# Second attention: PSUM banks dealt out anew, one for the projections and two for the maxima's scores

## The chip, the cores and the metric

The kernel runs on one core of one Trainium2 chip. A core has five engines that work side by side, each with its own queue that it takes in order: TensorE (PE in the profile; its weight loads are shown apart as PEld), VectorE (DVE), ScalarE (ACT), GpSimd (POOL), and SyncE (SP), which issues the DMAs here. Matmuls write to PSUM, which this program divides into eight banks of 128 partitions by 512 float32 values. A tile in a bank can be given to a new matmul when every instruction that reads the old tile is done.

The metric is the device time of the program in microseconds (us). Three runs of the kernel before took 915.53, 917.35 and 935.15 us; the median is 917.35.

## The reference

The program computes two transformer layers on x of 2 x 1024 x 128 in float32. Every sub-layer reads a layer norm of x, and its result is added to x:

```
x = x + attention0(ln(x))    # 16 heads of 8, softmax over 1024 keys
x = x + moe0(ln(x))          # 8 experts of 64, the best 2, and a shared expert
x = x + attention1(ln(x))    # 8 query heads, 4 key heads of 128, rotary, causal
x = x + moe1(ln(x))          # 16 experts of 128, the best 4
```

The change lies in attention1. Cut to what matters:

```
q = hidden @ Wq ; k = hidden @ Wk ; v = hidden @ Wv    # 8, 4 and 4 heads of 128
q = q * cos + rotate_half(q) * sin                     # k likewise
attn = softmax(causal(q @ k.T / sqrt(128)))            # two query heads share a key head
out  = (attn @ v) reshaped to (b, t, 1024) @ Wo
```

## The kernel before

**Stages.** The first attention takes the span up to some 370 us, the first feed-forward up to some 440, the second attention (`attn1`) up to some 805, and the second feed-forward the rest. They overlap at their ends: the scheduler moves independent work across.

**Units of the second attention.** For each batch b (2) and key head kv (4) there are four query chunks qc of 256 queries: 32 units, numbered 16 b + 4 kv + qc. Each unit serves the two query heads of its key head.

- *Projections* (`attn1_proj`, ten per key head): for each half i of the sequence one K (`kp`), two Q (`qp`), and two V (`vp`). `mm3` makes each float32 product out of three matmuls of high and low parts (its matmuls all have line 166). `vp` has six matmuls of 256 columns, since Wo has been multiplied into V's weights. K and Q go through `rope`: three VectorE operations read the projection's bank (lines 856 to 858), then GpSimd adds (859), ScalarE takes the high part (860), and GpSimd the low part (861). `vp` is copied to V by ScalarE (891).
- *Maxima* (`attn1_s`): for each of a unit's four pairs of query tile and head, one matmul per 512 keys writes scores to a tile `s` (915); VectorE reduces it to the row's maximum (920 for a part that isn't the last, 924 for the last with the causal mask). When the unit's four columns of m stand, `mt` turns them on TensorE (928). They reach the scores in one of two ways. In most units VectorE spreads them over rows (940), and a fourth matmul adds them to the scores (961). In the ten units of `APART` (3, 7, 14, 15, 22, 23, 26, 27, 30, 31) ScalarE copies them (931), one DMA stores them to memory (933), a second spreads them over all partitions (934), into `mb`, and VectorE subtracts `mb` from the scores (964).
- *Scores again, transposed* (`attn1_st`): for each key tile kt three matmuls to a tile `st` (954), the maxima as above, the exponential on ScalarE (966) into `pt`; on the diagonal GpSimd clears what is masked (970).
- *Products* (`attn1_av`): `pt` times V, with a column of ones that gives the sums, adds up in the tiles `o` (987), one for each query tile. At a tile's end come a reciprocal (994), ScalarE's scaling (998) and GpSimd's addition to x (1000).

**Order.** The loop in `attn1` emits this stepwise: one `st` step, then as many steps of the maxima's stream as keep it a fixed lead ahead (`lead < 13 + step*28//20`), then projections of the next key head by a rate, then one step of side work (weights and front ends of the second feed-forward), and the products one step late. From what is emitted, a scheduler makes each engine's own order, by its estimate of when operands and banks come free; only the first attention's TensorE order is fixed by hand (`manual_schedule`).

**PSUM banks in the second attention.** Eight banks are held by pools: `pst` has three, used by `pt(...)` for projections, `st`, `mt` and transposes in turn; `psy` has one (an `o` tile, later the feed-forward's sum); `a1s` has three for the maxima's scores; `a1o` has one for the other `o`. During the first feed-forward the four banks of `a1s` and `a1o` belong to its pool `f0u`.

The first five projections of the first key head are issued during the first feed-forward (`islice(g, 5)`).

Of the kernel before, what the change touches and what calls it, by code (L numbers as in the profile page):

```python
# [10 lines left out]
F32 = mybir.dt.float32  # L11
# [6 lines left out]
PSUM = bass.MemoryType.PSUM  # L18
# [6 lines left out]
CH = 512  # L25
# [13 lines left out]
def cols(t, w=128):  # L39
    return slice(t * w, (t + 1) * w)  # L40


def run(*gens):
    for g in gens:
        for _ in g:
            pass
# [26 lines left out]
class Net:  # L73
# [13 lines left out]
    def setup(self, ctx):  # L87
        nc = self.nc
        self.marks = {}
        self.fronts = set()  # L90
        self.nx = Counter()
        self.psu = None
        self.early = True
        self.const = self.pool(ctx, "const")
        self.small = self.pool(ctx, "small", 4)
        self.tok = self.pool(ctx, "tok", 2)
        self.hl = self.pool(ctx, "hl", 1)
        self.dram = self.pool(ctx, "dram", 2, DRAM)
        self.pst = self.pool(ctx, "pst", 3, PSUM)
        self.psy = self.pool(ctx, "psy", 1, PSUM)  # L100
        self.x = [self.const.tile([128, TPC, D], F32, name=f"x_{c}") for c in range(NCHUNK)]
        xin = self.a["x"].rearrange("(c t p) d -> c p t d", p=128, t=TPC)
        self.load_x = lambda c: nc.sync.dma_start(out=self.x[c], in_=xin[c])
        self.load_x(0)
        self.load_x(1)
        self.ident = self.const.tile([128, 128], F32, name="ident")
        make_identity(nc, self.ident)
        ones = self.tok.tile([128, CH], F32, tag="xT", name="ones")
        nc.vector.memset(ones, 1.0)
        self.zero = self.const.tile([128, 1], F32, name="zero")  # L110
        nc.vector.memset(self.zero, 0.0)
        self.ones_r = self.const.tile([128, 128], F32R, name="ones_r")
        nc.vector.tensor_copy(self.ones_r, ones[:, 0:128])
        self.ones = ones

    def pt(self, shape, name):
        return self.pst.tile(shape, F32, tag="t", name=name)
# [745 lines left out]
    def attn1_proj(self, b, kv, xh):  # L863
        nc, pp = self.nc, self.a1p
        K = [pp.tile([128, T], F32R, tag=f"K{k}", name=f"K{k}_{b}_{kv}") for k in range(2)]
        Q = [pp.tile([128, 2, T], F32R, tag=f"Q{k}", name=f"Q{k}_{b}_{kv}") for k in range(2)]
        V = pp.tile([128, 8, 2, 129], F32, tag="V", name=f"V_{b}_{kv}")

        def gen():
            nc.gpsimd.memset(V[:, :, :, 128:129], 1.0)  # L870
            for i in range(2):
                assert (b, i) in self.fronts
                xi = [w[:, i, :] for w in xh]
                p = self.pt([128, CH], f"kp_{b}_{kv}_{i}")
                self.mm3(p, [w[:, cols(kv)] for w in self.a1wk], xi)
                self.rope([w[:, cols(i, CH)] for w in K], p, i, f"k_{b}_{kv}_{i}")
                yield
                for h in range(2):
                    hh = 2 * kv + h
                    p = self.pt([128, CH], f"qp_{b}_{hh}_{i}")  # L880
                    self.mm3(p, [w[:, cols(hh)] for w in self.a1wq], xi)
                    self.rope([w[:, h, cols(i, CH)] for w in Q], p, i, f"q_{b}_{hh}_{i}")
                    yield
                for j in range(2):
                    p = self.pt([128, 2, 256], f"vp_{b}_{kv}_{i}_{j}")
                    for u in range(2):
                        self.mm3(
                            p[:, u, :], [w[:, i, cols(2 * j + u)] for w in xh], [w[:, kv, :] for w in self.a1wvo]
                        )
                    k0 = 4 * i + 2 * j  # L890
                    nc.scalar.copy(V[:, k0 : k0 + 2, :, 0:128], p.rearrange("p u (h d) -> p u h d", h=2))
                    yield

        return (K, Q, V), gen()

    def rows_apart(self, b, kv, qc):
# [311 lines left out]
def interleave(main, *sides, ratio=1):  # L1208
    s = Side()
    for g in sides:  # L1210
        s.add(g)
    for _ in main:
        s.step(ratio)
    s.drain()


def held(net, gen):
    while True:
        with ExitStack() as ctx:
            for ins in net.marks.values():  # L1220
                ctx.enter_context(net.tc.issue_after(ins.ins))
            if next(gen, gen) is gen:
                return
        yield


def later(gen, n):
    for _ in range(n):
        yield
    yield from gen  # L1230


def build(tc, aps, upto=4):
    n = Net(tc, aps)
    out = aps["out"].rearrange("(c t p) d -> c p t d", p=128, t=TPC)

    def dump():
        for c in range(NCHUNK):
            tc.nc.sync.dma_start(out=out[c], in_=n.x[c])

    with ExitStack() as ctx:
        n.setup(ctx)
        c1 = ctx.enter_context(ExitStack())
        cr = ctx.enter_context(ExitStack())
        n.f0wp = n.pool(cr, "f0w")
        w1 = n.attn1_weights(c1)
        with ExitStack() as c0:
            cb = c0.enter_context(ExitStack())
            n.attn0(
                c0, cb,  # L1250
                {266: lambda: w1, 456: lambda: n.ffn0_front(0, 1), 458: lambda: n.ffn0_front(2)}
                if upto > 1 else {},
            )
        if upto == 1:
            return dump()
        n.attn1_pools(c1)
        xh = [n.attn1_x(0), None]
        first, g = n.attn1_proj(0, 0, xh[0])
        n.f0k = n.pool(cr, "f0k", 1)
        gens = {"proj": islice(g, 5)}  # L1260
        for c in range(NCHUNK):
            gens[f"up{c}"] = n.ffn0_up(c)
            gens[f"down{c}"] = n.ffn0_down(c)
        gens["front3"] = n.ffn0_front(3)
        for i in range(2):
            gens[f"a1{i}"] = n.attn1_front(0, xh[0], i)
        with ExitStack() as c0:
            n.psu = n.pool(c0, "f0u", 4, PSUM)
            for word in ORDER.split():
                count, k = word.split("*")  # L1270
                for _ in range(int(count)):
                    next(gens[k], None)
            for k in gens:
                run(gens[k])
            n.psu = None
            n.early = False
        with ExitStack() as c2:
            with ExitStack() as c3:
                n.a1s = n.pool(c3, "a1s", 3, PSUM)
                n.a1o = n.pool(c3, "a1o", 1, PSUM)  # L1280

                def front1():
                    xh[1] = n.attn1_x(1)
                    yield from n.attn1_front(1, xh[1], 0)
                    yield from n.attn1_front(1, xh[1], 1)

                def weights1():
                    cr.close()
                    n.f1wp = n.pool(c2, "f1w")
                    yield from n.ffn1_weights()  # L1290

                plan = {10: [lambda: held(n, front1())]}
                if upto > 3:
                    plan[9] = [lambda: held(n, weights1())]
                    plan[18] = [lambda: n.ffn1_front(0)]
                    plan[21] = [lambda: n.ffn1_front(1)]
                    plan[30] = [lambda: later(n.ffn1_front(2), 3)]
                n.attn1(first, g, xh, plan)
            c1.close()
            if upto == 3:  # L1300
                return dump()
            wk1 = n.pool(c2, "f1k", 2)
            pu = n.pool(c2, "f1u", 4, PSUM)
            interleave(n.ffn1_back(0, wk1, pu, out), n.ffn1_front(3), ratio=1)
            run(n.ffn1_back(1, wk1, pu, out))
            run(n.ffn1_back(2, wk1, pu, out), n.ffn1_back(3, wk1, pu, out))
# [67 lines left out]
```

## Time and profile before

| | |
|---|---|
| median of three runs | 917.35 us (915.53 to 935.15) |
| profiled execution | 920.4 us, its span 918.7 us |
| TensorE busy | 882.5 us (96%) |
| VectorE busy | 795.8 us (87%) |
| ScalarE busy | 603.1 us (66%) |
| GpSimd busy | 307.7 us (33%) |
| mean granted clock of TensorE | 0.973 |
| DMA | 49.11 MB, mean 53 GB/s |

The profile is of one execution. A line such as `L964 DVE TENSOR_TENSOR pt<-st,mb` names the source line, the engine, the operation, and what it writes and reads. `A <- B: 3.0, 4, 2.2` in a list of waits says that A stood idle until B was done: 3.0 us in total, in 4 places, 2.2 us the longest. A matmul's busy time includes the filling of the array, so that matmuls which follow each other overlap in the records; the chain of waits shows them without that overlap. A float32 product `o` stands as two records, a product of high and low parts as one.

### The profile page before, as it was taken

To read this page: it belongs to the slowest core of one execution; us is meant where nothing else is said; L and a number is where in the kernel's file an instruction comes from. 1 tells how busy PE (TensorE), PEld (TensorE's weight loads), DVE (VectorE), ACT (ScalarE), POOL (GpSimd) and SP (SyncE) were. 2 spreads that over 40 slices of the span, in tenths; PEclk is the share of its full clock that TensorE was granted. 3 is DMA by queue.
4 is the path that set the end of the run, shared out by engine and by line. 5 is a ranking of instruction groups with operands and counts; after the bars stand their busy time and mean duration, and the time that the engine had idled before them with its cause. 6 is when DMAs were issued, how large, how long until landed. Compare 5 with 4: busy or idle time off the path is not lost.

```text
span 918.7 us, 17141 instructions
## 1 busy us (share of the span) xinstructions
PE 882.5 (96%) x6449; PEld 596.5 (65%) x6449; DVE 795.8 (87%) x1636; ACT 603.1 (66%) x1159; POOL 307.7 (33%) x392
## 2 busy tenths in 40 slices
PE   7999999999999999998899998999999989999997
PEld 5544444444443443467789897988888979866775
DVE  7899999999997998568787788899979996799987
ACT  5578998988986897864445545444445444578775
POOL 2620000000100000034664657375737463245331
PEclk9999999999997997899999999999999999999999
DMA  5890100011000000032000001000000000055462
GB/s 159 244 317 5 45 3 2 1 47 59 22 27 1 1 1 1 3 127 83 1 13 1 13 26 44 1 25 1 2 1 26 12 15 13 24 196 161 140 200 74
DMA packets 32043, 49.11 MB, mean 53 GB/s; under 512 B 4544, under 2 KB 10488, under 8 KB 31960
## 3 DMA queue, kind: packets, MB, share of 16 engines
q1 hardware_dynamic: 31960, 48.03, 16.2%
q8 instruction: 50, 0.82, 0.4%
q14 instruction: 33, 0.27, 0.1%
HBM read 38.36 MB, written 9.65 MB: 52 GB/s over the span
## 4 chain that ended last, share of the span: by engine, by line
PE 69%; DVE 15%; ACT 6%; issue 4%; POOL 2%; DMA 2%; SPq 0%; DVEq 0%; POOLq 0%; ACTq 0%
PE av L463 15%; PE st L443 13%; PE o L987 10%; PE st L954 8%; ACT pt L449 3%; PE s L915 3%; PE f1y L166 3%; PE f1p L166 2%; PE f0y L777 2%; PE st L961 2%; PE vp L166 1%; PE qp L166 1%; DVE s L924 1%; PE hot L410 1%; PE avt L484 1%
## 5 line engine op out<-in xcount | busy, mean ns | idle before, releaser
L404 DVE TENSOR_REDUCE mx<-s 128x2 f32<-128x1024 f32 x256 | 299.5, 1220 | 18.8 <-PE s L398 15.5
L449 ACT ACTIVATE pt<-st 128x512 f32<-128x512 f32 x476 | 252.5, 602 | 39.4 <-PE s L398 28.0
L463 PE MATMUL av<-pt,V 128*32 128x256 f32 x2048 | 169.3, 410 | 0.0
L987 PE MATMUL o<-V,pt 128*128 128x129 f32 x1152 | 156.3, 275 | 2.9 <-ACT pt L966 1.8
L398 PE MATMUL s<-KS,QM 24*128 24x512 f32 x512 | 156.0, 512 | 0.9 <-DVE KS L330 0.7
L987 PEld LDWEIGHTS o<-V,pt 128*128 128x128 f32 x1152 | 148.8, 191 | 11.6 <-ACT pt L966 2.3
L443 PE MATMUL st<-QX,KS 25*128 25x512 f32 x476 | 147.1, 513 | 1.6 <-DVE a1wvo L161 0.6
L954 PE MATMUL st<-Q,K 128*128 128x512 f32 (+1 forms) x480 | 136.1, 391 | 6.0 <-DVE rB_q L858 3.0
L443 PEld LDWEIGHTS st<-QX,KS 25*128 25x128 f32 x476 | 63.4, 188 | 101.8 <-ACT pt L449 50.4
L492 POOL TENSOR_TENSOR x<-x,ov 128x128 f32<-128x128 f32 x16 | 7.3, 455 | 284.4 <-DVE ov L489 284.4
L954 PEld LDWEIGHTS st<-Q,K 128*128 128x128 f32 x480 | 79.4, 189 | 17.9 <-DVE rB_q L858 4.8
L966 ACT ACTIVATE pt<-st 128x512 f32<-128x512 f32 x88 | 47.8, 545 | 59.5 <-PE st L961 50.2
L463 PEld LDWEIGHTS av<-pt,V 128*32 128x32 f32 x2048 | 43.2, 111 | 65.6 <-issue 62.4
L966 ACT ACTIVATE pt<-pt 128x512 f32<-128x512 f32 x72 | 43.3, 603 | 53.1 <-DVE pt L964 52.6
L398 PEld LDWEIGHTS s<-KS,QM 24*128 24x128 f32 x512 | 66.4, 187 | 10.8 <-DVE mx L404 5.4
L1000 POOL TENSOR_TENSOR x<-x,w 128x128 f32<-128x128 f32 x128 | 59.4, 464 | 27.6 <-ACT w L998 23.5
L915 PE MATMUL s<-K,Q 128*128 128x512 f32 (+2 forms) x192 | 63.2, 356 | 0.8 <-DVE m L924 0.7
L998 ACT ACTIVATE w<-o,rz 128x128 f32<-128x128 f32 x128 | 40.0, 365 | 34.2 <-DVE rz L994 31.1
L166 PE MATMUL f1y<-f1s,f1w 128*128 128x512 f32 x192 | 55.8, 412 | 3.9 <-POOL f1s L161 2.4
L964 DVE TENSOR_TENSOR pt<-st,mb 128x512 f32<-128x512 f32 x72 | 46.3, 646 | 9.9 <-PE st L954 6.0
L1177 DVE SCALAR_TENSOR_TENSOR f1f<-f1f,f1gb 128x512 f32<-128x512 f32 x64 | 48.4, 773 | 6.3 <-ACT f1f L1176 5.6
L970 POOL TENSOR_SCALAR_AFFINE_SELECT pt<-pt 128x256 f32<-128x256 f32 x64 | 26.5, 417 | 80.2 <-ACT pt L966 80.1
(238 smaller groups left out, 1554.0 us busy)
## 6 DMA issues: line engine op xcount, KB each, us to landing
f1gb<-f1gd SPq DMA_DIRECT2D x64, 256.0 KB
f0gb<-f0gd SPq DMA_DIRECT2D x32, 128.0 KB
kd<-k SPq DMA_DIRECT2D x12, 256.0 KB
qd<-q SPq DMA_DIRECT2D x12, 256.0 KB
QM<-qd SPq DMA_DIRECT2D x3, 1024.0 KB
mb<-md SPq DMA_DIRECT2D x10, 256.0 KB
KS<-kd SPq DMA_DIRECT2D x2, 1024.0 KB
KS<-kd SPq DMA_DIRECT2D x2, 768.0 KB
```

What stands on the lines that cost most here:

```text
L166: self.nc.tensor.matmul(out, lhsT=lhs[l], rhs=rhs[r], start=start and i == 0, stop=stop and i == 2)
L398: self.last_s = nc.tensor.matmul(ps[:, k, :], lhsT=QM[c][r, g, cols(t)], rhs=KS[c // 2][r, g, cols(h, CH)], start=True, stop=True)
L404: self.marks["V"] = nc.vector.tensor_reduce(mxs[n][:, h, 2 * pr : 2 * pr + 2, t : t + 1], ps, AX.X, ALU.max, negate=True)
L443: nc.tensor.matmul(ps, lhsT=KS[c // 2][32 * j : 32 * j + 25, g, cols(kt)], rhs=QX[n][32 * j : 32 * j + 25, :], start=True, stop=True,)
L449: self.marks["A"] = nc.scalar.activation(e, ps, AF.Exp, scale=INV_SQRT_D)
L463: return nc.tensor.matmul(avs[n][cols(j, 32), q], lhsT=V[c // 2][kt // 4][:, kt % 4, 4 * g + j, :], rhs=es[j][:, q], start=kt == 0 and i = ...
L915: nc.tensor.matmul(s[:, 0 : k1 - k0], lhsT=Q[0][:, h, cols(qt)], rhs=K[0][:, k0:k1], start=True, stop=True)
L954: k = nc.tensor.matmul(o, lhsT=K[l][:, cols(kt)], rhs=Q[r][:, :, q0 : q0 + w], start=i == 0, stop=apart and i == 2)
L966: k = nc.scalar.activation(e[:, :, 256 - w :], o, AF.Exp, scale=INV_SQRT_D)
L987: nc.tensor.matmul(acc[t][:, h, :], lhsT=e[:, h, cols(t)], rhs=V[:, kt, h, :], start=(kt == 0 and h == 0), stop=(kt == qt and h == 1),)
L1000: nc.gpsimd.tensor_add(xt, xt, w[:, h, :])
L1177: nc.vector.scalar_tensor_tensor(f, f, F7, gbs[e], ALU.min, ALU.mult)
```

## The change

Projections of the second attention that are emitted after the first feed-forward take their PSUM tiles from a new pool `a1q` with one bank. The pool `a1s` of the maxima's scores has two banks instead of three. The sum stays at eight. `st`, `mt` and the transposes stay in `pst` with its three banks, which no later projection shares. The first five projections are emitted before `a1q` exists and still use `pst`.

```diff
@@ setup
         self.psu = None
         self.early = True
+        self.a1q = None
@@ attn1_proj
+        def pt(shape, name):
+            return self.pt(shape, name) if self.a1q is None else self.a1q.tile(shape, F32, tag="p", name=name)
+
         def gen():
...
-                p = self.pt([128, CH], f"kp_{b}_{kv}_{i}")
+                p = pt([128, CH], f"kp_{b}_{kv}_{i}")
...
-                    p = self.pt([128, CH], f"qp_{b}_{hh}_{i}")
+                    p = pt([128, CH], f"qp_{b}_{hh}_{i}")
...
-                    p = self.pt([128, 2, 256], f"vp_{b}_{kv}_{i}_{j}")
+                    p = pt([128, 2, 256], f"vp_{b}_{kv}_{i}_{j}")
@@ build
-                n.a1s = n.pool(c3, "a1s", 3, PSUM)
+                n.a1s = n.pool(c3, "a1s", 2, PSUM)
+                n.a1q = n.pool(c3, "a1q", 1, PSUM)
                 n.a1o = n.pool(c3, "a1o", 1, PSUM)
```

Nothing else is edited. Every engine executes the same instructions as before; the scheduler, which knows the pools, sets them in another order from the end of the first feed-forward on.

## The prediction

> **What bounds the kernel now.** I read the page first, then busy time by stage, then who waited for whom inside the second attention, then the chain of waits.
>
> ```profile
> span 918.7 us, 17141 instructions
> ...
> PE 882.5 (96%) x6449; PEld 596.5 (65%) x6449; DVE 795.8 (87%) x1636; ACT 603.1 (66%) x1159; POOL 307.7 (33%) x392
> ```
>
> TensorE is the busiest engine, with VectorE behind it. Shares over a whole span mix stages, so the second attention is cut out (columns: stretch, length, busy us of PE, PEld, DVE, ACT, POOL, clock, DMA):
>
> ```profile
> 450.00:480.00 30.00, 29.43 (x185) 25.70 (x183) 24.54 (x59) 14.08 (x32) 21.42 (x27) 1.00 0.03 10
> 480.00:800.00 320.00, 310.09 (x2046) 278.12 (x2046) 273.55 (x740) 158.76 (x352) 178.69 (x260) 0.99 0.05 15
> ```
>
> PE is idle for 9.9 of 320 us: little is left to win here, while DVE, at 85%, has little room to be late. What PE waited for between 450 and 800 us (total, times, longest):
>
> ```profile
> PE st L954 <- DVE rB_q L858: 3.0, 4, 2.2
> PE st L954 <- ACT V L891: 1.7, 3, 0.9
> PE f1tp L170 <- DVE pt L964: 1.4, 1, 1.4
> PE o L987 <- ACT pt L966: 1.1, 1, 1.1
> PE st L954 <- DVE pt L964: 0.9, 1, 0.9
> ...
> PE qp L166 <- DVE rB_k L858: 0.6, 1, 0.6
> ```
>
> Rows one, two and the last are the shared `pst` banks: a tile waits until a projection's reader (VectorE's rope, ScalarE's copy into V) has left its bank. They come to 3.0 + 1.7 + 0.6 = 5.3 us. No row names a wait of PE for the maxima's scores.
>
> **How I count.** The change adds and removes no instruction; it changes which bank a tile gets, and so the order in which the scheduler puts the work. The changed program's order can be read. I lay PE's instructions out in that order and count the PE work between two tiles with these pieces of the chain (start, us, what):
>
> ```profile
> 525.51 0.71 PE vp L166 x6
> 526.22 0.70 PE st L954 x3
> ...
> 530.10 0.89 PE o L987 x8
> ```
>
> A 512-column matmul is thus 0.233 us, six of V 0.71, four whole products of `o` (two records each) 0.89. Where the work between two tiles of one bank is shorter than its reader needs, PE waits for the difference. The same count on the order of before shows how far to trust it.
>
> **Part 1, projections leave `pst`: minus 5.3 us.** `st` tiles and transposes now have all three banks. The 5.3 us above go. Next late on those tiles is the exponential, whose read (L966, mean 545 ns) the new order leaves ample work for, except in part 4.
>
> **Part 2, projections alone in one bank: plus 6.8 us.** Each projection waits until the one before it has been read. K's and Q's are read by three VectorE operations:
>
> ```profile
> L857 DVE TENSOR_TENSOR rB_q<-qp,sin x29: 692/692/695, 449.9 to 754.0; 64x512 f32<-64x512 f32 x29
> L858 DVE TENSOR_TENSOR rB_q<-qp,sin x29: 683/683/684, 450.6 to 754.7; 64x512 f32<-64x512 f32 x29
> L856 DVE TENSOR_TENSOR rA_q<-qp,cos x28: 661/680/693, 461.8 to 753.3; 128x512 f32<-128x512 f32 x28
> ```
>
> That is 0.68 + 0.69 + 0.68 = 2.06 us, 2.09 with the gaps between them. By the timeline the first began a median 0.55 us after the projection's last matmul (least 0.04, mean 0.95), so the bank is held 2.64 us (2.13 to 3.05) beyond it. In the new order the PE work between neighbouring projections falls short of 2.64 in 13 of 45 cases, by 10.3 us together (5.2 at 2.13, 16.9 at 3.05). The same count for before, with three shared banks, gives 5.0 us against 3.6 recorded (3.0 + 0.6). Two of them, 2.35 and 1.16, lie in the ramp before 450 us, where PE already sits out gaps of 0.4 to 1.3 us behind the first feed-forward; I take those as covered: 10.3 - 3.5 = 6.8. Without that cover it is 10.3. Behind a waiting projection in PE's queue stand `st` and `o`, so the wait stops everything. V's copies (0.59 us) are short once or twice: 0.3 us.
>
> **Part 3, maxima's scores in two banks: plus 1.0 us.** A score tile's bank is free when VectorE has reduced it, 0.28 to 0.76 us by width, once it comes to it. PE work between tile n and n+2 in the new order is short by 0.4 us in all if VectorE comes within 0.15 us, 2.2 within 0.5, 7.5 within 0.9 (the median delay of before, 0.86). For n and n+3 in the old order these counts are 0.6, 1.3 and 2.9, and the waits of PE show none; the weight loads (PEld) show 0.3. So VectorE is on time where it matters, and I take 1.0 net, between 0 and 7.
>
> **Part 4, the maxima come later: plus 5.7 us.** With two banks the scheduler sets each unit's scores later, and the transpose `mt` of its maxima closer to their use. For the ten units in `APART` the maxima go through memory before VectorE can subtract them. The last of these in before:
>
> ```profile
> 785.47 0.11 PE mt L928
> ...
> 787.12 3.61 DMA mb<-md
> ...
> 790.86 0.69 DVE pt L964
> ```
>
> From `mt` to this issue is 1.8 us; over the ten units 1.76 to 2.82, mean 2.25. With 3.61 for the landing the maxima arrive 5.86 us after `mt` (5.4 to 6.4), and with 0.68 for the first subtraction that unit's first `st` bank is free after 6.54. Three `st` of the unit fill `pst`; the tile after them must wait for that. PE work from `mt` to that tile, for units 3, 7, 14, 15, 22, 23, 26, 27, 30, 31: before 6.3, 6.9, 8.3, 6.8, 7.9, 6.8, 9.2, 6.9, 7.8, 6.2; after 5.2, 5.4, 6.8, 6.7, 7.1, 5.3, 12.6, 7.0, 5.7, 3.0. Short after: 1.3 + 1.1 + 1.2 + 0.8 + 3.5 = 8.0 (rounded terms add to 7.9). Before recorded 1.4 + 0.9 = 2.3 (rows three and five above, both unit 31). Net 5.7; 3.5 with the fastest chain, 9.5 with the slowest, nothing if the waits of part 2 already give the DMAs their time. For the other 22 units `mt` needs only VectorE's row product (L940, 664 ns), and the new order leaves 2.2 us or more but for the first unit, whose 1.1 us were 1.2 before.
>
> **Moved, at nothing.** SP's DMAs keep their order until 800 us; in the last feed-forward chunk 2's store of its routing weights goes behind eight loads of chunks 0 and 1, and chunk 3's behind one output store, each ahead of its own readers on that queue. VectorE is full behind the attention (37.9 of 40 us in 800 to 840), so anything pushed there would cost its length; but it has 200 rows of its order behind the last exponent's subtraction in both programs: nothing. GpSimd's and ScalarE's moved instructions follow their producers; those engines are 56% and 50% busy in 480 to 800, so they hide it; uncovered, one rope step is 1.3 us.
>
> **Clock.** The stage from 560 to 600 us had a mean clock of 0.96, so 40 x 0.04 = 1.6 us of clock lost; I leave this equal. The Trainium skill ("TensorE: Matmul & The Clock Gate", HAM oscillation) says that idle gaps beyond some 3.4 us halve TensorE's clock for a window; by it unit 31's wait would cost an estimated 1.7 us more and the sum would be 9.9. It speaks against the change, but this trace fits it poorly: in 40 to 380 us PE is busy 337.8 of 340 and the clock is still 0.94.
>
> **Sum.** -5.3 + 6.8 + 1.0 + 5.7 = +8.2 us. Against the profiled execution's 920.4 us that is 928.6; this execution lies 3 us over the median of the runs, 917.35, on which the same sum gives **925.5**.
>
> **Rivals.**
> - *Freed `st` banks win.* `st` runs ahead in threes ("st 0, st 1, st 2" before their products), ScalarE and VectorE get work early (VectorE sat 20.9 us waiting for scores), and the new waits hide in each other. For it: the scheduler placed each instruction where it took its bank for free, and many waits counted above are under 0.5 us. Against: PE's whole idle time is 9.9 us. Price: the 5.3 us and about half of the rest, 8 us: **909**.
> - *VectorE becomes the bound, slower.* Its queue is in order. VectorE work between the last maximum of such a unit and its first subtraction was 6.8, 8.9, 12.5, 13.4, 13.2, 12.1, 14.9, 13.0, 6.3, 4.0 us and is now 6.4, 4.8, 6.7, 7.2, 5.3, 3.1, 9.6, 6.6, 3.0, 4.0, where the maxima need about 6.6 (5.86 and a median 0.73 to `mt`). It then stands 13.0 us, against 1.7 recorded. Behind it are score reductions and ropes, which now hold the only two and the only one bank, so PE stands too. Price: 10 us on top of the forecast, and projections at the long end, 16.9 - 10.3 = 6.6: +25, **942**. It decides from the point where VectorE stands longer near these units than it had free there, 15% of its time (46.4 of 320 us).
> - *Nothing comes of it.* The waits merely change their bank: 5.3 us go and as much comes back, 917 within 4.
>
> **How the numbers follow.** Forecast 0.47, freed banks 0.20, VectorE 0.18, nothing 0.15. A measurement here tells about 2% (18 us) from no change. Faster by that (under 899) is the far tail of the first rival: 0.02. Slower by that (over 935.7) is the second and the forecast's upper tail: 0.18. Within: 0.80. The sum's own ends are -5.3 + 2 + 0 + 0 = -3 and -5.3 + 17 + 7 + 9.5 = +28; with the first rival on the low side the range is 908 to 943.
>
> **What would show it.** Right: PE's waits for `st` on `rB_q` and V vanish; waits of `qp` on `rB` of some 7 us appear; VectorE's wait for `mb` grows from 1.7 to 8 or more, and `st` or `o` on `pt` grow with it; PE's idle time in the stage goes from 10 to some 18 us. Wrong, and faster, if `mb` still lands in time: then `mt` came earlier than the order suggests, because PE lost time elsewhere. Wrong, and slower, if score matmuls wait for VectorE.

## The result, and the profile after

The changed kernel is slower: 1.0302 times the kernel before (95% interval 1.0224 to 1.0379; medians 953.0 against 924.0 us). The prediction was plus 0.9% and within 2%, in a range of 908 to 943 us; the time lies above it. The medians are of four executions each, while the ratio, here and below, leaves out executions that took over 1.5% longer than the fastest of their kernel, at a lower mean granted clock; two profiles below (the longer lead, and before with earlier projections) are of such executions, whose half clock lies mainly ahead of the stage that is compared.

The page of the changed kernel, the two lines that stood first for before:

```profile
span 936.6 us, 17149 instructions
...
PE 884.4 (94%) x6449; PEld 601.2 (64%) x6449; DVE 797.5 (85%) x1636; ACT 600.1 (64%) x1159; POOL 309.9 (33%) x392
```

The work is the same, PE 884.4 us against 882.5; the span is longer. The second attention again by stretches (columns as before: stretch, length, busy us of PE, PEld, DVE, ACT, POOL, clock, DMA):

```profile
450.00:480.00 30.00, 27.23 (x168) 23.04 (x167) 22.52 (x52) 12.06 (x29) 19.58 (x25) 0.98 0.03 10
480.00:820.00 340.00, 318.38 (x2057) 281.14 (x2056) 276.44 (x738) 155.03 (x349) 175.37 (x254) 0.99 0.04 14
```

PE now needs 340 us for what took 320 before (2057 matmul records against 2046) and is idle for 21.6 us of them, against 9.9. What PE waited for from 450 to 820 us (line numbers are by 1 to 4 higher than in before):

```profile
PE st L958 <- DVE pt L968: 5.1, 5, 3.1
PE s L919 <- DVE m L928: 3.0, 3, 1.8
PE vp L167 <- DVE rB_q L859: 2.3, 3, 1.6
PE s L919 <- DVE pm L924: 2.3, 3, 1.7
PE mt L932 <- DVE pt L968: 1.5, 3, 1.0
PE mt L932 <- DVE rw_f L124: 1.4, 1, 1.4
...
PE qp L167 <- DVE rB_q L859: 0.3, 1, 0.3
```

The waits of `st` on `rB_q` are gone, as they had to be. New are scores and `mt` that wait for VectorE, but none of the rows is large: projections wait for their one bank only some 3 us here. VectorE's own waits:

```profile
DVE s L928 <- PE s L919: 16.2, 16, 2.9
DVE pt L968 <- DMA mb<-md: 10.4, 5, 4.1
```

The second is the wait for the maxima on their way through memory, 1.7 us before. The five are 1.7, 0.9, 4.1, 2.6 and 1.1 us long, in units 14, 23, 27, 30 and 31. Around the second, the shortest, the chain of waits goes through the maxima and then stays on VectorE (start, us, what):

```profile
715.66 1.16 DMA md<-mb
716.89 3.03 DMA mb<-md
720.01 1.89 DVE pt L968 x3
721.90 0.60 DVE rA_k L857
722.51 0.69 DVE rB_k L858
723.22 0.68 DVE rB_k L859
724.02 0.55 DVE s L928
```

From there the chain stays on VectorE, with breaks of 0.7 us at most, up to 745 us. From 733 us on, part of that work is the routing of the second feed-forward (`tk_f`), so not all of it is a backlog that the maxima left.

**One measure for all versions.** The first attention has stretches of half clock that differ from one execution to the next: from 20 us to the second attention's start the granted clock was 0.5 for 41 us in the profile of before and for 17 in that of after, and that stage began 9.2 us earlier in after. Whole spans therefore understate the change. I compare the *stage*: from the last `f0gp` matmul of the first feed-forward to the last `o`. It took 380.7 us before and 408.3 after, 27.6 more: PE idle 31.5 instead of 16.1 us (+15.4); half clock inside it, whose lost half came to 8.5 instead of 1.7 us (+6.8); and 5.4 us in which PE counts as busy for longer over the same matmuls. Each stage below is that of one profiled execution.

### The profile page after: what moved, and what is told of

It reads as the page before. It is cut to its first block, busy times and chain, and to the rows that moved or that the text cites. A ratio compares the mean times of both kernels' runs of the same rounds, so it can differ in the third digit from the quotient of the medians.

```text
span 936.6 us, 17149 instructions
## 1 busy us (share of the span) xinstructions
PE 884.4 (94%) x6449; PEld 601.2 (64%) x6449; DVE 797.5 (85%) x1636; ACT 600.1 (64%) x1159; POOL 309.9 (33%) x392
## 4 chain that ended last, share of the span: by engine, by line
PE 65%; DVE 15%; ACT 6%; issue 5%; DMA 4%; POOL 3%; SPq 0%; DVEq 0%; POOLq 0%; ACTq 0%
PE av L464 14%; PE st L444 12%; PE o L991 8%; PE st L958 7%; ACT pt L450 3%; PE f1y L167 3%; PE f1p L167 2%; DMA mb<-md 2%; PE s L919 2%; DVE pt L968 2%; PE f0y L778 2%; DVE s L928 2%; PE vp L167 2%; PE qp L167 2%; PE st L965 1%
## 5 line engine op out<-in xcount | busy, mean ns | idle before, releaser
L464 PE MATMUL av<-pt,V 128*32 128x256 f32 x2048 | 163.5, 398 | 0.0
L399 PE MATMUL s<-KS,QM 24*128 24x512 f32 x512 | 152.4, 496 | 1.0 <-DVE KS L331 0.7
L444 PE MATMUL st<-QX,KS 25*128 25x512 f32 x476 | 144.4, 496 | 1.6 <-DVE a1wvo L162 0.6
L958 PE MATMUL st<-Q,K 128*128 128x512 f32 (+1 forms) x480 | 131.3, 387 | 5.2 <-DVE pt L968 5.1
L958 PEld LDWEIGHTS st<-Q,K 128*128 128x128 f32 x480 | 81.4, 191 | 17.9 <-DVE pt L968 7.1
L919 PE MATMUL s<-K,Q 128*128 128x512 f32 (+2 forms) x192 | 66.7, 374 | 6.3 <-DVE m L928 3.0
L1002 ACT ACTIVATE w<-o,rz 128x128 f32<-128x128 f32 x128 | 39.8, 364 | 41.5 <-DVE rz L998 34.2
L968 DVE TENSOR_TENSOR pt<-st,mb 128x512 f32<-128x512 f32 x72 | 44.7, 645 | 19.6 <-DMA mb<-md 10.4
L1181 DVE SCALAR_TENSOR_TENSOR f1f<-f1f,f1gb 128x512 f32<-128x512 f32 x64 | 50.4, 804 | 6.6 <-ACT f1f L1180 6.1
L167 PE MATMUL f1p<-f1x,f1w 128*128 128x512 f32 x192 | 53.4, 401 | 0.1
```

The lines of the kernel that those rows point to most:

```text
L167: self.nc.tensor.matmul(out, lhsT=lhs[l], rhs=rhs[r], start=start and i == 0, stop=stop and i == 2)
L399: self.last_s = nc.tensor.matmul(ps[:, k, :], lhsT=QM[c][r, g, cols(t)], rhs=KS[c // 2][r, g, cols(h, CH)], start=True, stop=True)
L444: nc.tensor.matmul(ps, lhsT=KS[c // 2][32 * j : 32 * j + 25, g, cols(kt)], rhs=QX[n][32 * j : 32 * j + 25, :], start=True, stop=True,)
L464: return nc.tensor.matmul(avs[n][cols(j, 32), q], lhsT=V[c // 2][kt // 4][:, kt % 4, 4 * g + j, :], rhs=es[j][:, q], start=kt == 0 and i = ...
L919: nc.tensor.matmul(s[:, 0 : k1 - k0], lhsT=Q[0][:, h, cols(qt)], rhs=K[0][:, k0:k1], start=True, stop=True)
L958: k = nc.tensor.matmul(o, lhsT=K[l][:, cols(kt)], rhs=Q[r][:, :, q0 : q0 + w], start=i == 0, stop=apart and i == 2)
```

## The experiments

The expectations name theories by letters, as they were formed; the main ones are **A**, the ten `APART` units' maxima come late through memory, VectorE stands and then lags; **B**, the single projection bank's hold; **C**, the two score banks; **F**, the scheduler's moving of the projections; **G**, any order but before's loses (each expectation words it anew); **H**, the banks themselves. "Rope waits" are PE's waits, for a bank, on the rope's operations (`rA`, `rB`); all sums of waits are over the stage.

### Each part alone, and the wait for the maxima

Two score banks alone, on before:

```diff
-                n.a1s = n.pool(c3, "a1s", 3, PSUM)
+                n.a1s = n.pool(c3, "a1s", 2, PSUM)
```

> The kernel before with two banks for the maxima's scores, projections still in the shared three; one bank lies idle. Theory A (the maxima of the ten units arrive too late through memory, VectorE stands and then is behind): in this program's order the PE work from mt to the tile that is blocked is 5.5, 5.9, 8.1, 6.9, 7.8, 6.7, 8.0, 7.1, 6.6 and 3.0 us, so only three or four units are short; 4 to 12 us slower than before, with mb waits of 2 to 6 us. Theory B (one bank for all projections is what costs): within 4 us of before. Theory C (two score banks stop PE by themselves, a score matmul waiting for VectorE): 18 us or more slower, with PE waits for the maxima's readers of 5 us or more.

Measured: 1.0042 (0.9968 to 1.0116), stage 383.4 us, PE idle 15.9. C falls, as long as the scheduler may set its own order; VectorE's wait for `mb` is 1.5 us, under A's 2 to 6.

The projections' own bank alone, with three score banks; the bank comes out of `st`'s three:

```diff
-        self.pst = self.pool(ctx, "pst", 3, PSUM)
+        self.pst = self.pool(ctx, "pst", 2, PSUM)
+        self.pst1 = self.pool(ctx, "pst1", 1, PSUM)
...
+                n.a1s = n.pool(c3, "a1s", 3, PSUM)
+                n.a1q = n.pst1
```

> Projections of the second attention in a bank of their own, but the scores keep three banks; the bank is taken from the shared three, so st and mt have two. Theory A: the work from mt to the blocked tile is 7.7, 7.1, 8.7, 7.5, 10.2, 7.0, 9.7, 6.3, 7.4, 4.8 us, longer than before, so no more than 8 us slower, mb waits under 3 us. Theory B: 18 us or more slower, PE waiting for rB of the projection before by 8 us or more. Theory C: within 5 us of before.

Measured: 1.0283 (1.0191 to 1.0376), stage 400.3, PE idle 26.1, rope waits 11.4 us. Nearly the whole loss is there without any change to the score banks. But `st` and `mt` have lost a bank here, and the waits that this may bring are there too (`st` for the subtraction 4.4 us, `o` for the exponential 3.2), so this run alone doesn't put the loss on the projections' bank.

The wait for `mb` taken out of both kernels; in the ten units VectorE subtracts the cosine table in place of the maxima:

```diff
-            res[(b, kv, qc)] = mb
+            res[(b, kv, qc)] = self.cos[:, 0:CH].rearrange("p (r q) -> p r q", r=4)
```

> The changed kernel, where the ten units of APART subtract a part of the table of cosines, which lies ready since the first attention, in place of their own maxima; the copy and both DMAs are still issued. So nothing waits for the maxima's way through memory. To be compared with the kernel before altered in the same way. Theory A: the difference between the two shrinks from some 27 us to under 10. Theories B and C: it stays at 18 us or more.

> The kernel before, altered in the same way: the ten units subtract a part of the table of cosines in place of their maxima. All theories: 0 to 5 us faster than the kernel before, whose VectorE waited 1.7 us for a DMA and whose PE waited 2.3 us behind it.

Measured: 1.0225 (1.0119 to 1.033) on the changed kernel, 1.0035 (0.9955 to 1.0115) on before. The distance between the two is 1.9 points without the wait and 3.0 with it. By the middle values A is a third of the loss, by the intervals it could be nothing: the most striking row of the profile after is not shown to be the main cause, and by the middle values it isn't.

### More lead, more projection banks, a shorter hold

> The changed kernel with the maxima's stream led by 19 steps in place of 13, so that mt stands 9 to 16 us of PE work ahead of the tile that its landing blocks (3 to 13 in the changed kernel). Theory A: mb waits vanish, 5 to 10 us faster than the changed kernel, still slower than before. Theory B: the projection waits stay and so does the rest, 15 to 25 us slower than before. If the lateness of VectorE behind the maxima were everything, the time would come back to before.

```diff
-                while lead < 13 + step * 28 // 20:
+                while lead < 19 + step * 28 // 20:
```

Measured: 1.0177 (1.0056 to 1.0298), PE idle 26.0. VectorE's wait for `mb` is gone from the list, as A wrote. By the middle values 1.25 points are won back, and 1.8% stays without that wait.

> Projections in two banks of their own in turn, st and mt in two, the maxima's scores in two. Against the kernel with one projection bank and two st banks (28 us slower than before) it gives a bank from the scores to the projections. Theory B, sharpened (one bank for projections, held until VectorE's three rope operations are done, ties TensorE and VectorE to each other): the waits of qp and vp for rB fall from 11 us to under 3 and the time comes back to within 8 us of before, although st has two banks and the scores two. Rival D (two banks for st are what costs in that experiment): 15 us or more slower than before, PE waiting for the subtraction and the exponential.

```diff
+            self.nq += 1
+            return (self.a1q, self.a1q2)[self.nq % 2].tile(shape, F32, tag="t", name=name)
...
+                n.a1q = n.pst1
+                n.a1q2 = n.pool(c3, "a1q2", 1, PSUM)
```

Measured: 1.0301 (1.022 to 1.0382), stage 402.9, PE idle 26.5. The second projection bank did not bring the time back, and the rope waits, which it should have removed, are still 7.4 us: with two banks the scheduler sets K's and Q's projections 14.7 us of PE work earlier than before did, and again close together. The run changes more than that one bank: `st` has two left, as in the run with the projections' own bank, and the scores have two; `st` waits 6.8 us for the subtraction and `o` 3.0 for the exponential, which is rival D's picture.

Next, ScalarE copies the projection out of its bank first and VectorE reads the copy, so that the bank is held for less:

```diff
-        nc.vector.tensor_mul(A, p, self.cos[:, cs])
-        nc.vector.tensor_mul(Bt[0:64], p[64:128], self.sin[64:128, cs])
-        nc.vector.tensor_mul(Bt[64:128], p[0:64], self.sin[0:64, cs])
+        nc.scalar.copy(A, p)
+        nc.vector.tensor_mul(Bt[0:64], A[64:128], self.sin[64:128, cs])
+        nc.vector.tensor_mul(Bt[64:128], A[0:64], self.sin[0:64, cs])
+        nc.vector.tensor_mul(A, A, self.cos[:, cs])
```

> The changed kernel, where ScalarE copies each K and Q projection to SBUF (into the tile of the first product) and the three rope operations read that copy, so that the one bank is free after about 0.6 us of ScalarE in place of about 2.1 of VectorE behind its queue. ScalarE gets 43 more copies of 0.6 us in this stage, 26 us where it was half idle. Theory B: PE waits for rB vanish, and the kernel comes to within 8 us of the kernel before with the same copies. Theory A (maxima through memory): nothing changes in the mb waits, the difference between the two stays at 15 us or more. Theory C (scores in two banks): likewise 15 or more, PE waiting for the maxima's readers.

> The kernel before with the same ScalarE copies. Projections leave the shared banks sooner, so the 3.6 us of waits behind rB go; ScalarE's copies stand in the way of exponentials. All theories: within 8 us of before; it is the control for the changed kernel with copies.

Measured: 1.0371 (1.0299 to 1.0443) on the changed kernel and 1.0285 (1.0196 to 1.0375) on before. The edit costs before 2.9% by itself, more than all theories allowed. The two are 0.9 points and 5.0 us of stage apart (414.5 against 409.5), and no wait of PE for `rB` is left in the changed one: that is B's side of its line (within 8 us; A and C wrote 15 or more). But the control moved as much as the effect that was looked for, so the pair supports B and doesn't decide it.

### Where the projections stand

The changed order has K's and Q's projections 5.5 us of PE work earlier than before's, on the mean. Tied in the changed kernel to the newest `st` step at which they are emitted, they stand where they stood (0.4 us later; V's some 3 us later):

```diff
+    def tied(self):
+        with ExitStack() as ctx:
+            if self.a1q is not None and len(self.sts1) > 1:
+                ctx.enter_context(self.tc.issue_after(self.sts1[-1].ins))
+            yield
```

> The changed kernel with one addition: a projection may not be issued before the st tile that was emitted last ahead of it. Banks are those of the changed kernel. Theory F (with a pool of their own the projections are no longer held in line with st, the scheduler puts K's and Q's projections earlier, by a mean 5.5 us of PE work in the changed kernel and by 4.4, 5.2 and 14.7 in the three other slow kernels with such a pool, against 0.2 in the one with two score banks and shared projections, which lost nothing; their ropes then take VectorE from the maxima and the subtractions): here their mean place is 0.4 us later than before, so the stage from the last routing transpose of the first feed-forward to the last product comes back to within 8 us of before's 379 (without the time lost at half clock), and the kernel to within 10 us of before. Theory B (the single bank itself): it stays 18 us or more slower, as the bank is the same. Theory G (two score banks and a projection pool together, whatever the order): likewise 15 or more.

Measured: 1.0356 (1.0283 to 1.0429), stage 413.7, PE idle 33.9. F falls as the main cause: with K's and Q's projections at their old place it is no faster.

Before, with its projections emitted earlier:

```diff
-                want = min(5, 2 * step) + 10 * k + (min(10, r * 10 // 12 + 1) if step >= 3 else 0)
+                want = min(5, 2 * step) + 10 * k + (min(10, r * 10 // 12 + 3) if step >= 3 else 0)
```

> The kernel before with its banks, only the rate at which projections are emitted is two ahead; K's and Q's then stand a mean 3.6 us of PE work earlier, mt stands where it stood. Theory F: the cause in small, without any change of banks: 6 to 15 us slower than before, PE waiting more for VectorE's readers. Theories B and G: within 5 us of before.

Measured: 1.0102 (1.0012 to 1.0192), stage 390.8, PE idle 20.1. With no change of banks, another order costs some 9 us, as F wrote and B and G did not: a third of what is to be explained.

Two score banks, and the freed bank added to the shared ones, every fourth tile in it:

```diff
+        if self.a1q is not None:
+            self.npt += 1
+            if self.npt % 4 == 0:
+                return self.a1q.tile(shape, F32, tag="t", name=name)
         return self.pst.tile(shape, F32, tag="t", name=name)
...
-                n.a1s = n.pool(c3, "a1s", 3, PSUM)
+                n.a1s = n.pool(c3, "a1s", 2, PSUM)
+                n.a1q = n.pool(c3, "a1q", 1, PSUM)
```

> Two banks for the maxima's scores, and the bank that this frees joins the shared ones in rotation: projections, st and mt share four. Theory F: projections stay in line (a mean 0.8 us earlier), so within 6 us of before; if the freed waits for a shared bank (5.3 us in before) count, up to 5 us faster. Theory B: the same. Theory G does not bear on it.

Measured: 1.012 (1.0067 to 1.0173), stage 395.3, PE idle 23.6. F and B, which wrote at most 6 us, both missed. Against the first run of all, this one only adds a bank, and its stage is 11.9 us longer; its largest wait is `st` on the subtraction, 8.3 us. No projection bank stands alone here, so an order that the scheduler sets can lose this much without one.

### Banks and order told apart

Up to here each change of banks also changed the order on every engine. The next four hold an order fixed: the program is first scheduled with one set of banks, and its order is then imposed on a program with another set, on all engines in three of them and on VectorE alone in one. In the traces of the three, the records of TensorE, VectorE, ScalarE and GpSimd stand in the same order, by operation, tile and shape, as in the version whose order they take.

```diff
+            for e, ks in (order or {}).items():
...
+                for a, b in zip(ks, ks[1:]):
+                    tc.add_manual_dep(
+                        emitted[e][b],
+                        emitted[e][a].name,
+                        mybir.DependencyInfo(mybir.DependencyClass.NoSync, mybir.DependencyReason.DATA),
+                        reason="order",
+                    )
```

> The changed kernel's banks (projections one, scores two), while every engine issues its instructions in exactly the order of the kernel before. This separates the banks from the order that the scheduler makes of them. In before's order the projections stand closer: PE work from one to the next is short of 2.64 us in 27 cases by 29.4 us (changed order: 14.1), and of three shared banks the same order was short by 5.0. Theory H (the banks themselves cost, the scheduler's new order only softens it): some 24 us of waits of qp and vp on rB and 2 to 5 of scores on maxima, 1.025 to 1.035 or more, stage 400 to 410 us; VectorE's wait for mb stays near 1.7 us, since mt stands where it stood. Theory G (the new order costs, and the banks' holds are mostly hidden by waits elsewhere): at most 1.012, stage 381 to 389, waits of qp and vp under 8 us. Between the two, the stage's excess over before (381 us) as a share of the 27.6 of the changed kernel says how much is banks.

Measured: 1.053 (1.0318 to 1.0742), stage 425.0, PE idle 47.7 us. (The 14.1 us given there for the changed order hold one pair, 3.8 us, whose second projection lies in the shared banks; without it, it is the 10.3 of the prediction.) The longest waits of PE in this version's stage:

```profile
PE vp L189 <- DVE rB_q L881: 12.5, 13, 2.2
PE s L944 <- DVE m L953: 11.7, 12, 2.0
PE qp L189 <- DVE rB_q L881: 9.3, 9, 2.3
PE s L944 <- DVE pm L949: 6.4, 6, 1.8
```

This is the price of the banks in the open: projections that wait for the rope to leave their bank (21.8 us), scores that wait for a maximum to leave theirs (18.1 us, where H had written 2 to 5), while before recorded 4.3 and 0.7. G, with at most 1.012 here, falls as the main cause. The changed kernel's own order is the better one for these banks.

With VectorE alone held to its old order and the others free:

> The changed kernel's banks, VectorE alone held to the order of the kernel before; the scheduler sets the other engines. The mt of the maxima goes 0.9 us earlier against before, scores 1.8 later, projections 1 to 3.4 later. If VectorE's order is what costs in the changed kernel (row products and subtractions queued behind late maxima): 1.00 to 1.012, VectorE's wait for mb under 5 us. Theory H (banks): PE work between projections is short of 2.64 us by 33.1, so 1.025 to 1.04. Theory G in its general form, that any order but before's own loses: 1.01 to 1.03 with waits spread over many rows.

Measured: 1.0594 (1.0412 to 1.0777), above H's range too; stage 438.5 us, of which half clock took 17.1, rope waits 25.9, score waits 3.4 us, VectorE's wait for `mb` 1.7. So VectorE's order, and the late `mb`, aren't needed for the loss either.

Two score banks alone in before's order:

> The kernel before with two score banks instead of three (projections still share the three of st), every engine held to exactly the order of the kernel before. The run before the last held the same order with both parts of the change and was 1.053, with 21.6 us of waits of vp and qp on rB_q and 18.1 us of scores on maxima. If two score banks cost by themselves once the scheduler can't give way: waits of scores on m and pm of 10 to 18 us, stage 391 to 400, 1.012 to 1.025. If these waits came only because the single projection bank holds PE and VectorE up in turn: under 5 us, stage 381 to 386, at most 1.008, and the 44 us of that run belong to the projection bank and what it sets off.

Measured: 1.0314 (1.0071 to 1.0557), stage 403.1, PE idle 34.2; its longest waits of PE:

```profile
PE s L944 <- DVE m L953: 14.2, 15, 2.0
PE s L944 <- DVE pm L949: 8.2, 8, 1.8
PE f0y L800 <- DVE f0h L784: 2.6, 2, 1.3
```

This lies over the upper ends of the expectation. The third score bank was worth 22.4 us of stage in before's order (403.1 - 380.7): PE is idle 18.1 us longer, with 21.7 us more of score waits and less of others, and 4.3 us lie in busy time. The scheduler, when it may reorder, hides nearly all of it (the first run, +2.7).

And the projections' bank added in exactly that first run's order, which hides the score banks:

> The changed kernel's banks, every engine held to the order that the scheduler made for two score banks alone (that version took 1.0042 of before, stage 383.4 us). So only the projections' single bank is new here. If that bank costs in this order what it cost in before's order (22 us of the 44): waits of vp and qp on rB 20 to 26 us, stage 403 to 410, 1.02 to 1.035, about the changed kernel's own 408.3 and 1.030; then the scheduler's new order in the changed kernel recovers little of the bank's hold, and only turns it into other waits. If the scores' 18 us come back as well because the ropes are late: stage 415 to 425, 1.04 to 1.055, and the changed order recovers some 10 us.

Measured: 1.0265 (1.0111 to 1.0418), stage 410.1, PE idle 37.4; its longest waits of PE:

```profile
PE qp L189 <- DVE rB_q L881: 16.2, 15, 2.3
PE vp L189 <- DVE rB_q L881: 10.4, 11, 2.3
PE st L983 <- DVE pt L993: 3.4, 1, 3.4
```

The runs together (stage, idle time, what half clock took of the stage, and waits, in us):

| score banks | projections | order | stage | PE idle | half clock | rope waits | score waits |
|---|---|---|---|---|---|---|---|
| 3 | shared | before's | 380.7 | 16.1 | 1.7 | 4.3 | 0.7 |
| 2 | shared | before's | 403.1 | 34.2 | 1.7 | 2.4 | 22.4 |
| 2 | one bank | before's | 425.0 | 47.7 | 8.5 | 21.8 | 18.1 |
| 2 | shared | its own | 383.4 | 15.9 | 3.4 | 1.8 | 2.3 |
| 2 | one bank | that of the row above | 410.1 | 37.4 | 6.8 | 26.6 | 2.3 |
| 2 | one bank | its own: the changed kernel | 408.3 | 31.5 | 8.5 | 4.6 | 5.3 |

In before's order the score bank costs 22.4 us and the projection bank another 21.9, of which 6.8 are half clock: 15.0 without it. With two score banks alone the scheduler's own order takes the first away (383.4); on that the projection bank puts 26.7 us, 23.3 without half clock. In both fixed orders only the bank is new, and the waits that come are those for the rope.

The last two rows bear on the changed kernel itself: its own order has 22 us less of rope waits than the order above it, and a stage only 1.8 us shorter. In their place stand waits of `st`, `mt` and `s` on a VectorE that is late, and the late `mb`. I read this as the hold of the one bank exchanged for other waits, not hidden; that is argued from the sizes, not shown. A rival remains: orders differ by themselves, by 10.1 us of stage with before's own banks (projections earlier) and by 14.6 with four shared banks, so part of the changed kernel's 27.6 us may be of that kind (6.7, 11.2 and 20.7 us without half clock).

## Why the prediction was wrong

**Part 2 failed, and with it "How I count".** One bank for the projections was put at +6.8 us, from the PE work between neighbours in the *changed* order, and at 16.9 at most. In the two orders that were held fixed this bank costs 21.9 and 26.7 us of stage, 15.0 and 23.3 without half clock. The count itself is of the right size for the waits, a quarter to a third too high: in before's order it gives 29.4 us where 21.8 were recorded, and in the order of the first run 33.2 against 26.6. But in the changed order the scheduler had already moved things to make these gaps long; what the move cost was charged nowhere. The count gave what was left to see (10.3; 4.6 recorded), not the price. A better figure was in reach: the same count on the old order.

**Part 3** (+1.0) agrees with what it says, two score banks with a free order: +2.7 us of stage, 1.0042, by its interval no change. Its ground, that VectorE is on time where it matters, holds only for an order that the scheduler may choose: in before's order the count with VectorE 0.9 us late gives some 13 us, and 22.4 were recorded.

**Part 4** (+5.7) had its mechanism right, and on PE about its size: VectorE's wait for `mb` rose from 1.7 to 10.4 us, "8 or more" was written, and `st` on the subtraction has 5.1 us. But without that wait the distance between the kernels shrinks by 1.1 of 3.0 points, and in the old order (the changed banks in before's order) a loss of 5.3% stands with that wait at 1.8 us.

**Part 1** (-5.3) is right as to the rows; but the waits removed were the mild form of the ones that came.

**Moved, at nothing** failed: another order alone, with before's banks, took 10.1 us more of the stage (projections earlier). What the changed order's own moves cost, apart from the bank, no run shows.

**Clock left equal** was off by 6.8 us in the profiled pair. In the 4 us ahead of each half-clock stretch of the stage PE had gaps: one of 2.2 us ahead of 572 in before; in after 1.5 and 1.3 ahead of 427, 1.6 ahead of 478, 1.7 and 0.7 ahead of 745, and three of 0.4 to 0.7 ahead of 693. The prediction set the Trainium skill's rule aside ("TensorE: Matmul & The Clock Gate", HAM oscillation: idle gaps over some 3.4 us). The length doesn't agree here: none of these gaps reaches 3.4 us, and the longest of after, 3.1 us at 808 (the wait in unit 31 that the prediction priced by that rule), was followed by no half clock at all. Nor does the sum of idle time settle it: with two score banks in before's order PE was idle for 34.2 us and half clock took 1.7, as in before with 16.1. So how much of the 6.8 us comes from the change stays open.

**The rivals.** The right side and nearly the right time, 942 where 945 would be 1.0302 of the median, came from "VectorE becomes the bound", at 0.18. Its picture, VectorE standing near the ten units and score and projection matmuls behind it, is in the profile after, and "wrong, and slower, if score matmuls wait for VectorE" is in the rows (5.3 us of score waits). Its price was built on the `mb` wait, though, which the runs make a minor part, so the near hit is partly luck. The sum's own upper end, +28, would have been 945; the range was ended at 943. "Freed `st` banks win" had nothing for it in any run.

**What stays open.** Why a free order hides nearly all of the score bank and next to nothing of the projection bank is only argued: a projection's bank waits for three VectorE operations, 2.1 us, a score's for one of 0.28 to 0.76. The 5.4 us by which PE's busy time grows I take for restarts after more gaps (4.3, 5.9 and 3.0 us in the three versions with a fixed order and all engines held, by the same sum), which isn't shown. Two versions weren't run: the changed order with before's banks, which would price the order alone, and before's banks with before's order imposed, which would price the imposing.

## What to carry to other kernels

Price a lost buffer on the order that was made without the loss, too: count there how long its next user would have waited. A scheduler's new order shows few such waits; here it showed 4.6 us of them in a kernel that lost 27.6. The old order's count is no forecast either: the score bank cost 22.4 us there and 2.7 when the scheduler could reorder. Take the two as a low and a high estimate, not as bounds. To tell banks from order, impose the old order on the new banks; then the waits stand under their own names.

## What was not expected

- The largest new row after (VectorE's wait for `mb`, 10.4 us) isn't needed for the loss. In before's order the same banks have that wait at 1.8 us, and lose 5.3%.
- In before's fixed order the third score bank and the projections' share of `st`'s banks were worth 22 us each, of a stage of 381 (the second 15 without half clock). A free order won nearly all of the one back and, by the stage, next to nothing of the other.
- In the second attention the granted clock fell to half after gaps on PE of 2.2 us and less. In the first attention it did so with no gap over 0.14 us in the 4 us ahead (at 77, 197, 282, 347, 374 us before; 175, 339, 362 after), for 41 us in one profiled execution and 17 in the other.
